# Attention over a sparse graph, edge by edge in place of dense with a mask

## The chip, the cores and the metric

The kernel runs on one core of a Trainium2 chip. The core has five engines with queues of their own: PE (TensorE, matmuls and transposes into PSUM), DVE (VectorE), ACT (ScalarE), POOL (GpSimd) and SP (SyncE, which issues DMAs here). Instructions stand in order on each engine and wait for one another through semaphores. The metric is the device time of one execution in microseconds (us), lower is better. Timed runs are not profiled; one further execution is profiled, and every duration below comes from it.

## What is computed

One layer of a graph neural network: layer norm and relu of x, then attention with 8 heads of 64 over the neighbours that `adj` allows, and x is added back. x is (16, 1024, 512) float32, `adj` is (1024, 1024) and the same for all 16 batches.

```
h = maximum(layernorm(x), 0)
q, k, v = (h @ W + b).reshape(b, n, 8, 64)            # for Wq, Wk, Wv of 512 x 512
scores = einsum('bihd,bjhd->bhij', q, k) / sqrt(64)
scores = scores + where(adj == 0, -1e9, 0)
out = einsum('bhij,bjhd->bihd', softmax(scores), v)
return x + out.reshape(b, n, 512)
```

The inputs make an adjacency with hubs: an edge (i, j) has the chance 0.0039 w_i w_j with w falling as the root of the index, and each token has an edge to itself. With the seed used there are 5,061 edges among 1,048,576 pairs; the token with the most has 66, the median token 4.

## The kernel before

`main_path` (lines 37 to 309) does the dense attention. A batch has 8 iterations of the loop at line 300: one for each of 4 pairs of heads (128 columns) and each half of 512 queries. An iteration goes over 8 tiles of 128 keys in `scores` (line 169): two matmuls of 64 rows by 512 queries (line 174), the mask added by DVE from PSUM (line 177), the exponential on ACT (line 178), and a running sum over the key tiles on POOL (lines 181 and 183). `weighted_sum` (line 185) multiplies with V for the iteration before (line 192), reduces the running sum on DVE (line 202), and loads the piece of x to be added. `row_sums` and `finish` (lines 212 and 224) make the inverse, transpose back on PE (line 229), divide on DVE (line 231), add x on POOL (line 236) and store from SP's queue (line 237).

The work of the next batch is spread over the iterations as fillers (line 245): x is loaded, `stats` takes mean and variance on DVE (lines 116 to 118) and the power on POOL (line 119), `norm` makes the shift on DVE (line 125) and the relu on ACT (line 126), `flip` transposes on PE (line 135) and copies on ACT (line 136), and `proj_k`, `proj_q` and `proj_v` do four matmuls of 512 columns each with a bias added (lines 143, 150 and 159). The order on PE, DVE, ACT and POOL inside this loop is the order in which the code is written (`manual_schedule`, line 299); only SP's is chosen by the scheduler.

`make_mask` writes the mask once, transposed by PE. Since no maximum is subtracted ahead of the exponential, `all_rows_fine` looks at the row sums at the end, and only if one is out of bounds does `general_path` run over everything again.

Of the kernel before, what the change touches and what calls it, by code (L numbers as in the profile page):

```python
# [19 lines left out]
F32 = mybir.dt.float32  # L21
BF16 = mybir.dt.bfloat16
# [12 lines left out]


def main_path(tc, x, adj, Wq, bq, Wk, bk, Wv, bv, out, sums):
# [4 lines left out]
    NH = N // 512  # L42
    TH = NT // NH
    DC = D // P
    ITS = DC * NH

    with ExitStack() as ctx:
        pool = lambda name, bufs=1, **k: ctx.enter_context(tc.tile_pool(name=name, bufs=bufs, **k))
        const = pool("const")
        xpool = pool("xpool", 5)  # L50
        hpool = pool("hpool", 4)
        kqpool = pool("kqpool", 2)
        vpool = pool("vpool", 2)
        ppool = pool("ppool", 12)
        apool = pool("apool", 2)
        work = pool("work", 2)
        small = pool("small", 4)
        psum = bass.MemoryType.PSUM
        ps_s = pool("ps_s", 3, space=psum)
        ps_a = pool("ps_a", 2, space=psum)  # L60

        X, HT, Q, K, V, MV, RSTD = {}, {}, {}, {}, {}, {}, {}

        def load_x(b, t):
            X[b, t] = xpool.tile([P, D], F32, tag="x", name=f"x_{b}_{t}")
            nc.sync.dma_start(X[b, t], x[b, ts(t, P), :])

        for t in range(2):
            load_x(0, t)

        ident = const.tile([P, P], F32, tag="ident", name="ident")
        make_identity(nc, ident)

        same = const.tile([P, P], F32, tag="same", name="same")
        own = const.tile([P, 2 * TH, 4], F32, tag="own", name="own")
        place = const.tile([P, 32], F32, tag="place", name="place")
        group = const.tile([P, 4], F32, tag="group", name="group")
        nc.vector.tensor_reduce(place, ident.rearrange("p (g q) -> p q g", q=32), AX.X, ALU.add)
        nc.vector.tensor_reduce(group, ident.rearrange("p (g q) -> p g q", q=32), AX.X, ALU.add)
        nc.vector.tensor_copy(same.rearrange("p (g q) -> p g q", q=32), place[:, None, :].to_broadcast([P, 4, 32]))  # L80
        nc.vector.tensor_copy(own, group[:, None, :].to_broadcast([P, 2 * TH, 4]))
        minus_half = const.tile([P, 1], F32, tag="mhalf", name="minus_half")
        nc.gpsimd.memset(minus_half, -0.5)

        W = {}
        bias = {}
        for name, w, vec in (("k", Wk, bk), ("q", Wq, bq), ("v", Wv, bv)):
            W[name] = const.tile([P, DC, H * HD], F32, tag="w" + name, name="w" + name)
            nc.sync.dma_start(W[name], w.rearrange("(c p) n -> p c n", p=P))  # L89
            if name == "v":  # L90
                bias[name] = const.tile([P, H * HD], F32, tag="bv", name="bv_rows")
                src = bass.AP(tensor=vec.tensor, offset=vec.offset, ap=[[0, P], [1, H * HD]])
            else:
                bias[name] = const.tile([P, DC], F32, tag="b" + name, name=f"b{name}_cols")
                src = vec.rearrange("(c p) -> p c", p=P)
            nc.sync.dma_start(bias[name], src)  # L96


        mask = const.tile([P, NT, N], BF16, tag="mask", name="mask")

        def make_mask(qt):
            row = ppool.tile([P, N], F32, tag="p", name=f"adj_{qt}")
            nc.sync.dma_start(row, adj[ts(qt, P), :])
            nc.vector.tensor_scalar(row, row, 0.0, -BIG * HD**0.5, op0=ALU.is_equal, op1=ALU.mult)
            for g in range(NT // 4):
                pt = ps_a.tile([P, 4, P], F32, tag="acc", name=f"pmask_{qt}_{g}")
                for j in range(4):
                    nc.tensor.transpose(pt[:, j, :], row[:, ts(4 * g + j, P)], ident)  # L108
                nc.scalar.copy(mask[:, 4 * g : 4 * g + 4, ts(qt, P)], pt)
# [381 lines left out]
```

## Time and profile before

| | us |
|---|---|
| median of 3 runs (3400.69 to 3402.33) | 3401.33 |
| the profiled execution, its own time | 3402.22 |
| its span | 3400.4 |
| ACT, activations of line 178: busy | 1082.3 |
| DVE, mask of line 177: busy | 1182.2 |
| POOL, running sum of lines 181 and 183: busy | 302.9 + 1811.3 |

The page of a profile gives for each engine the busy time in the span, the chain of work that ended last (followed back from the last instruction, with shares by engine and line), and groups of instructions: line, engine, operation, output<-inputs with their shapes, count | busy time in us, mean ns of one | idle time of the engine just ahead of them and what ended it. Windows give the busy time of each engine in a stretch, the granted TensorE clock, the DMA engines' busy share and GB/s. A float32 matmul can have more than one record for one instruction of the program, so records are set against the loops of the code.

### The profile page before, as it was taken

What the parts mean: (1) busy time and instruction counts of PE and PEld (TensorE: products, weight loads), DVE (VectorE), ACT (ScalarE), POOL (GpSimd) and SP (SyncE); (2) the same over time, 40 slices, a digit from 0 to 9 for tenths busy, and PEclk for the clock granted to TensorE, in tenths of its full rate; (3) what the DMA queues carried; (4) which work ended last, traced back from release to release, by engine and by line L of the source; (5) the groups of instructions that cost most, each with busy time, mean ns of one, the idle gap of its engine ahead of it and who ended that gap; (6) DMA issues with size and microseconds to landing.
All of it is one profiled execution on the core that took longest, in us unless ns stands there. A gap on an engine that the chain in (4) does not pass through costs nothing.

```text
span 3400.4 us, 33496 instructions
## 1 busy us (share of the span) xinstructions
PE 3359.0 (99%) x12610; PEld 1365.5 (40%) x12610; DVE 1998.0 (59%) x2450; ACT 1414.9 (42%) x1553; POOL 2338.3 (69%) x1160
## 2 busy tenths in 40 slices
PE   7999999999999999999999999999999999999997
PEld 3344444444443444344434443444444434444433
DVE  3556556565665656656556565665566556565455
ACT  3444434444443444344444443444444434444343
POOL 0777767676776677667666776777677767676777
PEclk9999999999999999999999999999999999999999
DMA  3011101111010111001100010101101110110000
GB/s 136 28 28 33 34 28 28 34 32 32 25 38 25 32 31 35 28 25 31 38 28 29 25 41 28 28 28 35 31 29 30 36 28 29 32 31 19 19 25 26
DMA packets 157704, 110.49 MB, mean 32 GB/s; under 512 B 7392, under 2 KB 138464, under 8 KB 157536
## 3 DMA queue, kind: packets, MB, share of 16 engines
q1 hardware_dynamic: 157536, 108.30, 10.7%
q8 instruction: 100, 1.64, 0.2%
q14 instruction: 68, 0.56, 0.1%
HBM read 74.72 MB, written 33.55 MB: 32 GB/s over the span
## 4 chain that ended last, share of the span: by engine, by line
PE 97%; DVE 1%; POOL 1%; issue 1%; SPq 0%; DMA 0%; ACT 0%; DVEq 0%; POOLq 0%; ACTq 0%
PE ps L174 27%; PE po L192 26%; PE pq L150 13%; PE pk L143 13%; PE pv L159 13%; PE pht L135 2%; PE pot L229 2%; PE pr L215 1%; POOL a L183 1%; DVE p L177 0%; PE pmask L108 0%; DMA x<-in_x_dram 0%; SPq L89 0%; DVE st L116 0%; SPq L96 0%
## 5 line engine op out<-in xcount | busy, mean ns | idle before, releaser
L183 POOL TENSOR_TENSOR a<-a,p 128x1024 f32<-128x1024 f32 x768 | 1811.3, 2359 | 782.8 <-ACT p L178 732.6
L177 DVE TENSOR_TENSOR p<-ps,mask 128x1024 f32<-128x1024 f32 x1024 | 1182.2, 1217 | 750.7 <-PE ps L174 750.7
L178 ACT ACTIVATE p<-p 128x1024 f32<-128x1024 f32 x1024 | 1082.3, 1057 | 770.8 <-DVE p L177 714.4
L174 PE MATMUL ps<-qT,kT 64*128 64x512 f32 x4096 | 953.2, 603 | 5.3 <-DVE p L177 5.2
L192 PE MATMUL po<-p,v 128*64 128x512 f32 x4096 | 907.1, 595 | 1.5 <-DVE picked L219 1.5
L174 PEld LDWEIGHTS ps<-qT,kT 64*128 64x128 f32 x4096 | 365.1, 186 | 486.7 <-issue 346.2
L192 PEld LDWEIGHTS po<-p,v 128*64 128x64 f32 x4096 | 282.8, 137 | 609.7 <-issue 540.4
L181 POOL TENSOR_TENSOR a<-p,p 128x1024 f32<-128x1024 f32 x128 | 302.9, 2366 | 237.4 <-ACT p L178 237.4
L204 ACT COPY ot<-po 128x512 f32<-128x512 f32 x128 | 75.0, 586 | 938.9 <-PE po L192 938.9
L150 PE MATMUL pq<-hT,wq 128*128 128x512 f32 x1024 | 464.4, 596 | 0.0
L143 PE MATMUL pk<-hT,wk 128*128 128x512 f32 x1024 | 455.3, 597 | 0.0
L159 PE MATMUL pv<-wv,hT 128*128 128x512 f32 x1024 | 454.4, 597 | 0.0
L159 PEld LDWEIGHTS pv<-wv,hT 128*128 128x128 f32 x1024 | 189.9, 190 | 215.7 <-issue 215.7
L143 PEld LDWEIGHTS pk<-hT,wk 128*128 128x128 f32 x1024 | 189.7, 190 | 215.2 <-issue 215.0
L150 PEld LDWEIGHTS pq<-hT,wq 128*128 128x128 f32 x1024 | 184.5, 190 | 212.2 <-issue 198.5
L151 DVE TENSOR_SCALAR qT<-pq,bq_cols 128x512 f32<-128x512 f32 x128 | 96.1, 751 | 235.0 <-PE pq L150 235.0
L125 DVE SCALAR_TENSOR_TENSOR shift<-mv,rstd 128x1 f32<-128x1 f32 x128 | 226.3, 1777 | 2.6 <-POOL rstd L119 2.6
L231 DVE TENSOR_TENSOR o<-pot,inv 128x512 f32<-128x512 f32 x128 | 87.9, 686 | 190.6 <-PE pot L229 190.2
L160 DVE TENSOR_TENSOR v<-pv,bv_rows 128x512 f32<-128x512 f32 x128 | 87.9, 687 | 170.6 <-PE pv L159 170.6
L126 ACT ACTIVATE x<-x,shift,rstd 128x512 f32<-128x512 f32 x128 | 102.3, 811 | 174.7 <-DVE shift L125 174.5
L236 POOL TENSOR_TENSOR o<-o,xr 128x512 f32<-128x512 f32 x128 | 163.4, 1277 | 0.6 <-DVE o L231 0.6
L202 DVE TRANSPOSE_TENSOR_REDUCE rs<-a 128x32 f32<-128x1024 f32 x128 | 158.0, 1234 | 9.8 <-POOL a L183 9.8
(40 smaller groups left out, 845.5 us busy)
## 6 DMA issues: line engine op xcount, KB each, us to landing
x<-in_x_dram SPq DMA_DIRECT2D x128, 256.0 KB, 3.1
xr<-in_x_dram SPq DMA_DIRECT2D x128, 256.0 KB, 3.1
out_dram<-o SPq DMA_DIRECT2D x128, 256.0 KB, 2.4
adj<-in_adj_dram SPq DMA_DIRECT2D x8, 512.0 KB, 7.1
wk<-in_L_gnn_Wk_dram SPq DMA_DIRECT2D x1, 1024.0 KB, 8.7
wq<-in_L_gnn_Wq_dram SPq DMA_DIRECT2D x1, 1024.0 KB, 10.5
wv<-in_L_gnn_Wv_dram SPq DMA_DIRECT2D x1, 1024.0 KB, 11.9
bv_rows<-in_L_gnn_bv_dram SPq DMA_DIRECT2D x1, 256.0 KB, 8.6
```

The lines of the kernel that those rows point to most:

```text
L125: nc.vector.scalar_tensor_tensor(shift, mv[:, 0:1], -1.0, rstd, op0=ALU.mult, op1=ALU.mult)
L143: nc.tensor.matmul(acc, W["k"][:, c, ts(p, P)], HT[b, hf][:, c, :], start=(c == 0), stop=(c == DC - 1))
L150: nc.tensor.matmul(acc, W["q"][:, c, ts(p, P)], HT[b, hf][:, c, :], start=(c == 0), stop=(c == DC - 1))
L159: nc.tensor.matmul(acc, HT[b, hf][:, c, ts(tt, P)], W["v"][:, c, :], start=(c == 0), stop=(c == DC - 1))
L174: nc.tensor.matmul(ps[:, r, :], K[b, p][rows, ts(kt, P)], Q[b, p, qh][rows, :], start=True, stop=True)
L177: nc.vector.tensor_tensor(pr, ps, m[:, None, :].to_broadcast([P, 2, 512]), ALU.add)
L178: nc.scalar.activation(pr, pr, AF.Exp, scale=HD**-0.5)
L181: nc.gpsimd.tensor_tensor(ACC[i], PR[i, 0], pr, ALU.add)
L183: nc.gpsimd.tensor_tensor(ACC[i], ACC[i], pr, ALU.add)
L192: nc.tensor.matmul(po[rows, :], V[b][:, kt, p * P + r * HD : p * P + r * HD + HD], pr[:, r, :], start=(kt == 0), stop=(kt == NT - 1),)
L202: nc.vector.tensor_reduce(RS[i], acc, AX.X, ALU.add, apply_transpose=True)
L236: nc.gpsimd.tensor_tensor(o, o, XR.pop(i), ALU.add)
```

## The change

The dense attention on the main path is replaced by one that touches only edges. The dense general path stays behind the check at the end.

Once, before the loop: the degree of each token is counted, tokens are ranked by degree (highest first) with comparisons on DVE, and `perm` lists the tokens in this order. All later tiles of 128 tokens are in sorted order. The rows of `adj` are fetched in this order by indirect DMA, and each row's neighbours are found as the largest entries of a row that holds 1024 - rank where there is an edge (`max` gives eight at a time; `match_replace` removes them for the tile of the hubs). Tile t keeps at most `CAPS[t]` neighbours a token; a hub's further neighbours are cut in pieces of 5, and 128 extra rows ("tile -1") hold one piece each; the matrix `owner` says whose. Slots without a neighbour point to row 1023 and get the mask. The number of used slots and of edges go into `cover`, which the check at the end compares.

In each batch: x is fetched in sorted order by indirect DMA; statistics, relu, transposes and projections are as before in kind, but K and V (bias added on DVE for both) are stored to a DRAM tile of 1024 rows of 1024 floats, and q is projected when its tile comes. Then 11 units follow, each some slots of a tile: `gather` issues one indirect DMA a slot on POOL (128 rows of 4 KB: K and V of a neighbour), `score` multiplies K with q, reduces over 64 to 8 heads and adds the mask on DVE, then the exponential on ACT; `weigh` multiplies V with the weights, on ACT for units 0, 1 and 2 (one activation for each slot and head), on DVE for the others; `add_up` sums the slots by matmuls with the identity into PSUM, or, for units 5, 8 and 9, by a reduce on DVE and one matmul; `finish` sums the weights, divides, adds x on POOL, and scatters the rows to `out` by indirect DMA from POOL. There are three buffers for gathered rows. A unit's `weigh` and `add_up` are written after the `score` of the next one.

```
+CAPS = (11, 8, 6, 5, 4, 4, 3, 2)
+PIECE = 5
+PIECES = 17
...
+UNITS = ((7, 0, 2), (6, 0, 3), (5, 0, 4), (4, 0, 4), (3, 0, 5), (2, 0, 6), (1, 0, 4), (1, 4, 4), (0, 0, 6), (-1, 0, 5), (0, 6, 5))
...
+        gpool = pool("gpool", 3)
...
+        def load_x(n):
+            b, t = tile_at(n)
+            X[n] = xpool.tile([P, D], F32, tag="x", name=f"x_{b}_{t}")
+            nc.gpsimd.indirect_dma_start(
+                out=X[n][:], out_offset=None, in_=x_rows, in_offset=on(ap=perm[:, t : t + 1], axis=0), element_offset=b * N * D
+            )
...
+        def proj_kv(n):
...
+            for j, name in enumerate("kv"):
+                pt = ps_kv.tile([P, D], F32, tag="pkv", name=f"p{name}_{b}_{t}")
+                project(pt, name, n)
+                nc.vector.tensor_tensor(kv[:, j, :], pt, bias[name], ALU.add)
+            nc.sync.dma_start(KV[b][ts(t, P), :], kv.rearrange("p j d -> p (j d)"))
...
+        def gather(i):
...
+            G[i] = gpool.tile([P, UMAX, 2, D], F32, tag="g", name=f"g_{b}_{u}")
+            for s in range(count):
+                nc.gpsimd.indirect_dma_start(
+                    out=G[i][:, s].rearrange("p j d -> p (j d)"),
+                    out_offset=None,
+                    in_=KV[b][:],
+                    in_offset=on(ap=index[:, c + s : c + s + 1], axis=0),
+                )
...
+        def score(i):
...
+            k = G[i][:, :count, 0, :]
+            nc.vector.tensor_tensor(k, k, Q[b, t][:, None, :].to_broadcast([P, count, D]), ALU.mult)
...
+            nc.vector.tensor_reduce(w, k.rearrange("p s (h d) -> p s h d", h=H), AX.X, ALU.add)
+            nc.vector.tensor_tensor(w, w, mask[:, c : c + count, None].to_broadcast([P, count, H]), ALU.add)
+            nc.scalar.activation(w, w, AF.Exp, scale=HD**-0.5)
...
+        ON_ACT = (0, 1, 2)
...
+            if u in ON_ACT:
+                for s in range(count):
+                    for h in range(H):
+                        nc.scalar.mul(v[:, s, h, :], v[:, s, h, :], w[:, s, h : h + 1])
+            else:
+                nc.vector.tensor_tensor(v, v, w[:, :, :, None].to_broadcast([P, count, H, HD]), ALU.mult)
+
+        BY_REDUCE = (5, 8, 9)
...
+            if u in BY_REDUCE:
+                r = work.tile([P, D], F32, tag="r", name=f"r_{b}_{u}")
+                nc.vector.tensor_reduce(r, v.rearrange("p s d -> p d s"), AX.X, ALU.add)
+                terms = [r]
+            else:
+                terms = [v[:, s, :] for s in range(count)]
+            for k, term in enumerate(terms):
+                nc.tensor.matmul(
+                    acc,
+                    owner_t if t < 0 else ident,
+                    term,
...
+        def ahead(n):
+
+            if n + 3 < tiles:
+                load_x(n + 3)
+            if n + 2 < tiles:
+                stats(n + 2)
+            if n + 1 < tiles:
+                flip(n + 1)
+            proj_kv(n)
+            if n + 2 < tiles:
+                norm(n + 2)
...
+        LEAD = 2
+        with tc.manual_schedule(engines={mybir.EngineType.PE, mybir.EngineType.DVE, mybir.EngineType.Activation, mybir.EngineType.Pool}):
+            go_ahead(NT + LEAD)
...
             for i in range(total):
...
+                score(i)
+                if i:
+                    weigh(i - 1)
+                go_ahead(NT * (b + 1) + LEAD + NT * passed // SLOTS)
...
+                        queries(nb, nt)
+                if i:
+                    add_up(i - 1)
+                if i + 2 < total:
+                    gather(i + 2)
...
+                        finish(pb, home)
```

Three places show how the engines' order moves. In the rows a number after x is a count of like instructions in a row; names are the tiles of the code, with a number that tells buffers apart.

POOL before, one iteration in the middle of the program (`a` is the running sum of the weights `p`, `o` the result to which x is added):

```order
L236 TENSOR_TENSOR o_2440<-o_2440,xr_2373 128x512
L181 TENSOR_TENSOR a_2456<-p_0_2447,p_1_2453 128x1024
L183 TENSOR_TENSOR a_2456<-a_2456,p_2_2461 128x1024
L183 TENSOR_TENSOR a_2456<-a_2456,p_3_2468 128x1024
L119 TENSOR_TENSOR rstd_1_2504<-rstd_1_2504,minus_half 128x1
L183 TENSOR_TENSOR a_2456<-a_2456,p_4_2516 128x1024
```

POOL of the changed kernel, two units in the middle of the second batch (`g` is the buffer of a unit, `x` a tile in sorted order):

```order
L306 DMA g_4_1459<-kv_628,index 128x1024 x5
L386 TENSOR_TENSOR o_6_1469<-o_6_1469,x_6_544 128x512
L387 DMA out_dram<-o_6_1469,perm 16384x512
L154 DMA x_1_1510<-in_x_dram,perm 128x512
L166 TENSOR_TENSOR rstd_2_1514<-rstd_2_1514,minus_half 128x1
L306 DMA g_5_1555<-kv_628,index 128x1024 x6
```

The running sums are gone from POOL, and what SP issued before (loads of x, stores of the result) stands there now, with the gathers, in one queue with the power and the addition of x.

DVE of the changed kernel, from the mask of unit 2 to the division of the tile before it, whose weighing is on ACT:

```order
L323 TENSOR_TENSOR w_5_2020<-w_5_2020,mask 128x32
L163 BN_STATS st_3_2050<-x_3_1894 128x6
L164 BN_AGGR mv_3_2051<-st_3_2050 128x2
L165 TENSOR_SCALAR rstd_3_2052<-mv_3_2051 128x1
L198 TENSOR_TENSOR kvt_5_2064<-pk_5_2065,bk_rows 128x512
L198 TENSOR_TENSOR kvt_5_2064<-pv_5_2071,bv_rows 128x512
L173 SCALAR_TENSOR_TENSOR shift_3_2078<-mv_3_2051,rstd_3_2052 128x1
L298 TENSOR_TENSOR pq_4_2082<-pq_4_2082,bq_rows 128x512
L369 TENSOR_REDUCE sums<-w_6_1977 128x8
L377 TENSOR_SCALAR sums<-sums 128x8
L379 RECIPROCAL inv_6_2100<-sums 128x8
L381 TENSOR_TENSOR o_6_2102<-acc_6_2088,inv_6_2100 128x512
```

Before, eight instructions of line 177 stood in each iteration and the division followed a transpose; now the division (line 381) stands behind the next unit's score and waits for PE's sum of the unit before.

PE before, in one iteration (`po` is the weighted sum):

```order
L135 MATMUL pht_3_3946<-ident,x_3_3574 128x128 x4
L150 MATMUL pq_1_1_3953<-hT_1_3016,wq 128x512 x4
L192 MATMUL po_3959<-p_0_3788,v_2833 64x512 x2
L192 MATMUL po_3959<-p_1_3794,v_2833 64x512 x2
L192 MATMUL po_3959<-p_2_3802,v_2833 64x512 x2
```

PE of the changed kernel, two units (`acc` is the sum of a tile's slots):

```order
L182 MATMUL pht_4_1424<-ident,h_4_1293 128x128 x4
L188 MATMUL pk_5_1432<-wk,hT_5_1275 128x512 x4
L188 MATMUL pv_5_1438<-wv,hT_5_1275 128x512 x4
L188 MATMUL pq_4_1449<-wq,hT_4_796 128x512 x4
L359 MATMUL acc_6_1455<-g_1_1304,ident 128x512 x3
L182 MATMUL pht_3_1519<-ident,h_3_1447 128x128 x4
L188 MATMUL pk_4_1527<-wk,hT_4_1429 128x512 x4
```

The scores and the dense weighted sum are gone; a unit's sum (line 359) stands behind the projection of a tile of the next batch and of the next q, and ahead of the next transposes.

More of the change, by code (lines that the diff above doesn't have):

```diff
@@ L75, in main_path @@
[L75 to L80, printed above, removed]
@@ L224, in finish, with project @@
[L224 to L230 removed]
+            HT[n] = htpool.tile([P, DC, P], F32, tag="hT", name=f"hT_{b}_{t}")
+            nc.scalar.copy(HT[n], pt)
+        def project(pt, name, n):
+            for c in range(DC):
+                nc.tensor.matmul(pt, HT[n][:, c, :], W[name][:, c, :], start=(c == 0), stop=(c == DC - 1))
@@ new lines, in main_path, with queries @@
+        Q, G, WT, ACC = {}, {}, {}, {}
+        def queries(b, t):
+            pt = ps_q.tile([P, D], F32, tag="q", name=f"pq_{b}_{t}")
+            if t >= 0:
+                project(pt, "q", nth(b, t))
+                HT.pop(nth(b, t))
+            else:
+                nc.tensor.matmul(pt, owner, Q[b, 0], start=True, stop=True)
+                Q[b, t] = pt
+                return
+            if t == 0:
+                q = Q[b, t] = work.tile([P, D], F32, tag="q0", name=f"q0_{b}")
+            else:
+                q = Q[b, t] = pt
+            nc.vector.tensor_tensor(q, pt, bias["q"], ALU.add)
```

452 lines of the change are left out of this document (248 added, 204 removed).

## The prediction

> **What bounds the kernel now.** Read first the busy shares and the chain of the profile's page, then its groups of instructions.
>
> ```profile
> span 3400.4 us, 33496 instructions
> PE 3359.0 (99%) x12610; PEld 1365.5 (40%) x12610; DVE 1998.0 (59%) x2450; ACT 1414.9 (42%) x1553; POOL 2338.3 (69%) x1160
> ...
> PE 97%; DVE 1%; POOL 1%; issue 1%; SPq 0%; DMA 0%; ACT 0%; DVEq 0%; POOLq 0%; ACTq 0%
> ...
> L174 PE MATMUL ps<-qT,kT 64*128 64x512 f32 x4096 | 953.2, 603 | 5.3 <-DVE p L177 5.2
> L192 PE MATMUL po<-p,v 128*64 128x512 f32 x4096 | 907.1, 595 | 1.5 <-DVE picked L219 1.5
> ...
> L143 PE MATMUL pk<-hT,wk 128*128 128x512 f32 x1024 | 455.3, 597 | 0.0
> ```
>
> TensorE is busy 99% of the span and makes up 97% of the chain: the time is PE's work. 953 + 907 = 1860 us of it are the dense scores and the dense weighted sum, over all 1024 x 1024 pairs of tokens, of which the mask leaves 5,061. The change can only win there. One unit is needed for the rest: line 143 is reached 512 times (16 batches, 4 head pairs, 2 halves, 4 chunks of D), and the row counts 1024 records and 455.3 us, so a 128x512 float32 matmul of the program costs **0.89 us** of PE.
>
> The whole main path is replaced, so I build the new time from its stages. The sum is held against the profiled execution, 3402.2 us with a span of 3400.4; the median of the runs is 3401.33, the same within 0.03%.
>
> **DVE per batch.** A batch now is 11 units with 48 slots; a slot is 128 gathered rows.
>
> ```profile
> L177 DVE TENSOR_TENSOR p<-ps,mask 128x1024 f32<-128x1024 f32 x1024 | 1182.2, 1217 | 750.7 <-PE ps L174 750.7
> L160 DVE TENSOR_TENSOR v<-pv,bv_rows 128x512 f32<-128x512 f32 x128 | 87.9, 687 | 170.6 <-PE pv L159 170.6
> L231 DVE TENSOR_TENSOR o<-pot,inv 128x512 f32<-128x512 f32 x128 | 87.9, 686 | 190.6 <-PE pot L229 190.2
> L116 DVE BATCH_NORM_STATS2 st<-x 128x6 f32<-128x512 f32 x128 | 84.1, 657 | 14.9 <-DMA x<-in_x_dram 14.9
> L222 DVE RECIPROCAL inv<-sums 128x8 f32<-128x8 f32 x128 | 26.0, 203 | 4.5
> L220 DVE TENSOR_REDUCE sums<-picked 128x8 f32<-128x32 f32 x128 | 23.8, 186 | 4.4
> L117 DVE BATCH_NORM_AGGREGATE mv<-st 128x2 f32<-128x6 f32 x128 | 23.2, 182 | 4.2
> L118 DVE TENSOR_SCALAR rstd<-mv 128x1 f32<-128x1 f32 x128 | 19.6, 153 | 4.3
> L425 DVE TENSOR_REDUCE c_both<-sums 128x1 f32<-128x1024 f32 x1 | 1.2, 1210 | 0.0
> L78 DVE TENSOR_REDUCE place<-ident 128x32 f32<-128x128 f32 x1 | 0.4, 358 | 0.0
> L79 DVE TENSOR_REDUCE group<-ident 128x4 f32<-128x128 f32 x1 | 0.3, 276 | 0.0
> ```
>
> 512 elements take 687 ns and 1024 take 1217: 0.53 us for each 512 and 0.155 us an instruction; the reduce fits (1210). So: q times K, 48 slots in 11 instructions, 48 x 0.53 + 11 x 0.155 = 27.1. The reduce to 8 heads, the same, 27.1. Weights times V for the units that stay on DVE, 39 slots in 8, 21.9. Summing by reduce in units 5, 8 and 9, 17 slots in 3, 9.5, with strided reading: line 78 takes 82 ns more than line 79 for the same 128 elements, at most 0.64 ns each, so between 0 and 5.6 more; I take 2. Bias of K and V, 16 x 0.687 = 11.0; of q 5.5; division 8 x 0.686 = 5.5. Statistics 8 x (0.657 + 0.182 + 0.153) = 7.9 and the shift 1.2; mask, sums, clamps, reciprocals (0.15 to 0.2 each) 6.8. Together **125.5 us**, against 1998 / 16 = 125 before: DVE gains nothing.
>
> **PE per batch.** K, V and q of 8 tiles, 96 matmuls, one for the moved queries, 34 for the sums: 131 x 0.89 = 116.6, plus 32 transposes.
>
> ```profile
> L135 PE MATMUL pht<-ident,x 128*128 128x128 f32 x512 | 87.1, 296 | 20.6 <-ACT x L126 20.3 <-ACT hT L136 0.3
> ```
>
> These cost 87.1 / 512 = 0.17 each, 5.4. Together **122 us**, where it was 3359 / 16 = 210.
>
> **POOL and the DMA queues per batch.** POOL issues 48 gathers, 8 loads of x and 8 scatters, all 64 indirect DMAs that no row shows.
>
> ```profile
> L183 POOL TENSOR_TENSOR a<-a,p 128x1024 f32<-128x1024 f32 x768 | 1811.3, 2359 | 782.8 <-ACT p L178 732.6
> L236 POOL TENSOR_TENSOR o<-o,xr 128x512 f32<-128x512 f32 x128 | 163.4, 1277 | 0.6 <-DVE o L231 0.6
> L119 POOL TENSOR_TENSOR rstd<-rstd,minus_half 128x1 f32<-128x1 f32 x128 | 69.9, 550 | 30.7 <-DVE rstd L118 30.7
> ...
> 1.68 0.43 SPq L89 DMA_DIRECT2D wk<-in_L_gnn_Wk_dram  x1
> ...
> 8.11 1.94 SPq L96 DMA_DIRECT2D bv_rows<-in_L_gnn_bv_dram  x1
> ...
> 16.00:18.00 2.00, 0.00 (x0) 0.00 (x0) 0.61 (x1) 0.00 (x0) 0.00 (x0) 1.00 1.06 406
> 32.00:34.00 2.00, 1.91 (x14) 1.34 (x14) 1.00 (x2) 1.67 (x4) 0.00 (x0) 1.00 1.04 398
> ```
>
> Bounds for one issue: 0.43 us (SP's, of a plain load) to 2.36 (POOL's longest row). I take 1.28, POOL's row for one 128x512 tile, since 128 addresses have to be worked out by that engine. POOL: 64 x 1.28 + 8 x (1.277 + 0.55) = 96.5 us. The accumulations of line 183 go. Bytes: 48 x 0.52 + 8 x (0.26 + 0.52 + 0.26) = 33.6 MB a batch; both windows of full queues move about 400 GB/s, and the first still carries bv_rows, one 2 KB row read 128 times (issued at 8.11), as the padding here reads row N-1. That is 84 us. The stores of K and V wait in SP's queue for DVE; only later stores stand behind them.
>
> So no engine has more than 126 us in a batch, where before it was 210. What remains is who waits for whom. A gather waits on POOL for its buffer, freed by the sum three units earlier; behind it stand the add of x, the scatter, the next load and the next power, for which DVE's shift waits, but DVE first has a score to do (5 to 7 us), which covers it.
>
> **Waits on DVE, the first: ACT.** In units 0, 1 and 2 the weighing is 16, 24 and 32 activations of 64 elements.
>
> ```profile
> L178 ACT ACTIVATE p<-p 128x1024 f32<-128x1024 f32 x1024 | 1082.3, 1057 | 770.8 <-DVE p L177 714.4
> L204 ACT COPY ot<-po 128x512 f32<-128x512 f32 x128 | 75.0, 586 | 938.9 <-PE po L192 938.9
> L126 ACT ACTIVATE x<-x,shift,rstd 128x512 f32<-128x512 f32 x128 | 102.3, 811 | 174.7 <-DVE shift L125 174.5
> ...
> 6.31 1.52 ACT L126 ACTIVATE x<-x,shift,rstd 128x512 f32<-128x512 f32 x2 [1.35 <-DVE shift L125]
> ```
>
> 1024 against 512 elements is 0.47 us, so 64 with a scale per partition take about 0.811 - 0.41 = 0.40; two in a row start 0.71 apart, 0.1 less: 0.30 (bounds 0.17, from line 204's fixed part, and 0.40). That is 4.8, 7.2 and 9.6 us, then 2, 3 and 4 matmuls (1.8, 2.7, 3.6), before DVE can divide. In between DVE has 1.2 us of its own (q bias, small reduces) after unit 0 and 3.8 (statistics and K/V bias too) after the others: it waits 5.4 + 6.1 + 9.4 = **21 us**. **The second: PE in turns.** In a unit with a tile to project PE has 0.7 + 7.1 + 3.6 + about 4 = 15 us, DVE 12 to 14. About 2 us in six units, and 3 for the small matmul of finish(b, 0) that stands behind a projection: **15 us**.
>
> **The third: DVE against POOL.**
>
> ```profile
> 1999.22 2.19 DVE L125 SCALAR_TENSOR_TENSOR shift<-mv,rstd 128x1 f32<-128x1 f32 x1
> ...
> 1999.04 7.22 POOL L183 TENSOR_TENSOR a<-a,p 128x1024 f32<-128x1024 f32 x3
> ...
> L125 DVE SCALAR_TENSOR_TENSOR shift<-mv,rstd x128: 145/2182/2255, 6.1 to 3121.2; 128x1 f32<-128x1 f32 x128
> ```
>
> The shift has two SBUF operands and one element: 145 ns at best, 2.19 us here, ending as POOL's first addition ends. About 30 such instructions a batch remain (masks, weighing, shifts). If an indirect issue holds them as an addition does, 30 x half of 1.28 x POOL's share 0.6 is 11 us; if not, none. I take **4**. The Trainium skill, SBUF — State Buffer, section Who interferes with whom, says that a two-input DVE instruction contends only with a GpSimd instruction that reads SBUF. By that the additions hold it, as the 2.19 us show, and an issue that reads no tensor would not: the term would be 0 and the time 64 us less.
>
> **The fourth: PE's rate after idle.**
>
> ```profile
> 2003.71 0.60 PE L229 MATMUL pot<-ident,ot 128*128 128x128 f32 x4
> ...
> 3388.65 0.61 PE L215 MATMUL pr<-rs,same 128*128 128x32 f32 x2 [3.49 <-DVE rs L202]
> ...
> 3389.64 1.08 PE L229 MATMUL pot<-ident,ot 128*128 128x128 f32 x4 [0.38 <-DVE picked L219]
> ```
>
> Four transposes take 0.60 us in the stream and 1.08 after PE had been idle 3.49 us. PE will idle that long while ACT weighs, some four times a batch; a few us at half rate cost 1 to 2 us each time, mostly beside DVE: **5**.
>
> **The sum.** 125.5 + 21 + 15 + 4 + 5 = 170.5 us a batch, x 16 = 2728. Ahead of the loop, sorting and lists: 63 DVE instructions on 1024 elements at about 1.24, 45 small ones at 0.16, and some 15 us of loads and hand-overs, 100; then ten tiles of projection, PE 7.8 plus 1.5 of turns each, 93. The last batch projects nothing (-30), last store and check +10. 100 + 93 + 2728 - 30 + 10 = about **2900 us**.
>
> **The rivals.**
> - *Nearly no waiting.* ACT's multiplications at 0.17 and PE ahead of DVE: 140 us a batch, 2415. For it: four engines with slack. Against: one unit of lead, and PE and DVE within 4 us of each other. 0.20.
> - *POOL becomes the bound, slower than before.* Place: POOL's queue, 64 issues. With 15 us of buffer waits a batch is 64 c + 30; at c = 2.36 that is 181, 3070 us. It equals before where a batch takes (3402 - 173) / 16 = 202 us, c = 2.7; at 3.2 it is 235, 3930. For it: POOL's rows are the slowest per element. Against: nothing is added up. 0.15, 0.06 of it slower.
> - *PE stays at half rate.* With half of its matmuls at it PE needs 183 us, with 20 of waits 203 and 3420; with all, 244 and more. For it: the 1.08 against 0.60, and an engine that falls to 72% busy with gaps. Against: as it slows the gaps close. The Trainium skill, TensorE: Matmul & The Clock Gate, section HAM oscillation — how this bites in real kernels, says gaps over about 3.4 us drop the clock to half each time; the 3.49 us here agree, though the column of the granted clock reads 1.00. 0.09, 0.07 of it slower.
> - *Gathers at half bandwidth.* At 200 GB/s 168 us of transfers and 10 of waits, 3020; slower below 175 GB/s. Against: 398 and 406 in both full windows. 0.08, 0.03 slower.
> - *The sparse path isn't taken.* More edges than slots would add the dense general path to all this. The seed's adjacency has 5,061 edges, tile maxima of 66, 8, 6, 5, 4, 3, 3, 2 (caps 11 and extra pieces, 8, 6, 5, 4, 4, 3, 2) and 101 of 128 extra pieces: it fits. 0.02.
>
> **How the numbers follow.** My forecast, 2900 within 200, has 0.46. The range reaches down into the first rival and up into the others: 2450 to 3450 leaves out some 0.2. Slower: 0.06 + 0.07 + 0.03 + 0.02 = 0.18; within 0.2% (7 us, about what a measurement of this kernel can tell from no change) 0.03; faster 0.79.
>
> **What would show it.** DVE near 2000 us and PE near 1960 busy, neither above 75%; DVE idle before the division, released by PE's sums; the indirect issue on POOL near 1.3 us; L336 near 0.3 us; DMA share near a half. I am wrong in a step if POOL or the DMA leads the chain, if matmuls of 128x512 last clearly longer than 597 ns, or if a batch takes under 145 us.

## The result, and the profile after

The changed kernel takes **2872.61 us** (median of 4 runs, 2870.18 to 2873.86) where the kernel before takes 3401.01 beside it: a ratio of 0.8446, 95% interval 0.8431 to 0.846. The forecast was 2900, within 2450 to 3450.

The page of the changed kernel, the same parts as were shown of before:

```profile
span 2872.0 us, 16724 instructions
PE 2074.3 (72%) x4759; PEld 912.0 (32%) x4759; DVE 2161.5 (75%) x2287; ACT 485.2 (17%) x1590; POOL 1462.3 (51%) x1298
...
PEclk9998898888989888888989888897988889798776
...
q0 software_dynamic: 132224, 474.02, 49.3%
...
PE 43%; DVE 36%; issue 8%; ACT 6%; DMA 6%; POOL 1%; DVEq 0%; SPq 0%; ACTq 0%; POOLq 0%
```

PE was 99% busy and 97% of the chain. Now no engine is busy more than 75%, and the chain changes hands between PE and DVE. The granted clock is mostly at eight or nine tenths and ends at six; before, it was at nine or more in every slice:

```profile
PEclk9999999999999999999999999999999999999999
```

The queue of POOL's DMAs (the gathers, and the loads of x and scatters with them) takes 49% of the DMA engines.

The groups of instructions, with shapes apart, in the same columns:

```profile
L306 POOL DMA_INDIRECT g<-kv,index x768 | 865.9, 1127 | 988.1 <-PE acc L359 418.1 <-DVE r L354 227.6 <-issue 184.7
L336 ACT ACTIVATE g<-g,w 128x64 f32<-128x64 f32 x1152 | 280.0, 333 | 0.6 <-ACT w L324 0.2
L354 DVE TENSOR_REDUCE r<-g 128x512 f32<-128x3072 f32 x32 | 170.5, 5327 | 0.6
L322 DVE TENSOR_REDUCE w<-g 128x48 f32<-128x3072 f32 x32 | 107.3, 3353 | 1.1
L359 PE MATMUL acc<-r,ident 128*128 128x512 f32 x64 | 65.9, 1133 | 460.4 <-DVE sums L369 242.3 <-DVE r L354 218.1
L323 DVE TENSOR_TENSOR w<-w,mask 128x32 f32<-128x32 f32 x64 | 59.4, 928 | 2.2
L323 DVE TENSOR_TENSOR w<-w,mask 128x40 f32<-128x40 f32 x32 | 6.4, 200 | 1.1
```

Three rows stand out. The strided sum (L354) needs 5.33 us for 3072 elements where the reduce along rows (L322) needs 3.35: 0.64 ns more an element. The matmul that takes its result is at 1133 ns a record, almost twice the 600 of the stream, after 460 us of idle time. And the mask of 32 elements takes 928 ns, of 40 elements 200.

Nine batches: the window runs from PE's small matmul for the moved queries (ahead of unit 9) in the first batch, at 307.1 us, to the same matmul in the tenth, at 1812.5, which is 167.3 us for each. First the busy time of PE, PEld, DVE, ACT and POOL, granted clock, DMA share and GB/s; then what DVE waited for:

```profile
307.10:1812.50 1505.40, 1152.59 (x2666) 508.73 (x2665) 1169.16 (x1207) 269.97 (x891) 820.76 (x721) 0.87 0.59 201
```

```profile
DVE o L381 <- PE acc L359: 111.4, 54, 5.3
DVE shift L173 <- POOL rstd L166: 80.5, 45, 4.6
DVE pq L298 <- PE pq L188: 56.5, 27, 2.7
DVE sums L375 <- PE p_more L374: 30.4, 9, 3.4
DVE g L318 <- DMA g<-kv,index: 25.8, 9, 3.5
DVE q L298 <- PE pq L188: 7.0, 9, 1.0
DVE kvt L198 <- PE pv L188: 5.5, 18, 1.4
```

DVE works 1169 / 9 = 129.9 us a batch and waits (317.1 us in these rows) 35.2; 2 us are small gaps. That the rows add up to the batch says nothing yet of which of them is worth anything: a wait that goes may only make room for the next. The experiments ask that.

### The profile page after: what moved, and what is told of

It reads as the page before. It is cut to its first block, busy times and chain, and to the rows that moved or that the text cites. A ratio compares the mean times of both kernels' runs of the same rounds, so it can differ in the third digit from the quotient of the medians.

```text
span 2872.0 us, 16724 instructions
## 1 busy us (share of the span) xinstructions
PE 2074.3 (72%) x4759; PEld 912.0 (32%) x4759; DVE 2161.5 (75%) x2287; ACT 485.2 (17%) x1590; POOL 1462.3 (51%) x1298
## 4 chain that ended last, share of the span: by engine, by line
PE 43%; DVE 36%; issue 8%; ACT 6%; DMA 6%; POOL 1%; DVEq 0%; SPq 0%; ACTq 0%; POOLq 0%
PE acc L359 13%; PE pq L188 10%; PE pk L188 9%; PE pv L188 8%; DVE g L318 8%; DVE r L354 8%; DVE w L322 7%; DVE g L338 5%; ACT g L336 5%; DMA g<-kv,index 5%; PE pht L182 2%; DVE w L323 1%; POOL g L306 1%; DVE st L163 1%; ACT h L175 1%
## 5 line engine op out<-in xcount | busy, mean ns | idle before, releaser
L306 POOL DMA_INDIRECT g<-kv,index x768 | 865.9, 1127 | 988.1 <-PE acc L359 418.1
L359 PE MATMUL acc<-g,ident 128*128 128x512 f32 x992 | 500.4, 646 | 111.0 <-ACT g L336 64.5
L188 PE MATMUL pk<-wk,hT 128*128 128x512 f32 x1024 | 497.2, 631 | 0.0
L188 PE MATMUL pq<-wq,hT 128*128 128x512 f32 x1024 | 489.1, 623 | 0.0
L359 PE MATMUL acc<-r,ident 128*128 128x512 f32 x64 | 65.9, 1133 | 460.4 <-DVE sums L369 242.3
L322 DVE TENSOR_REDUCE w<-g 128x32 f32<-128x2048 f32 (+4 forms) x160 | 391.4, 2446 | 5.5
L338 DVE TENSOR_TENSOR g<-g,w 128x2048 f32<-128x2048 f32 (+2 forms) x112 | 306.9, 2740 | 0.0
L318 DVE TENSOR_TENSOR g<-g,pq 128x2048 f32<-128x2048 f32 (+4 forms) x128 | 291.5, 2278 | 0.1
L336 ACT ACTIVATE g<-g,w 128x64 f32<-128x64 f32 x1152 | 280.0, 333 | 0.6 <-ACT w L324 0.2
L381 DVE TENSOR_TENSOR o<-acc,inv 128x512 f32<-128x512 f32 x128 | 88.6, 692 | 226.2 <-PE acc L359 223.8
L354 DVE TENSOR_REDUCE r<-g 128x512 f32<-128x3072 f32 (+1 forms) x48 | 241.9, 5039 | 0.6
L387 POOL DMA_INDIRECT out_dram<-o,perm x128 | 207.6, 1622 | 37.3 <-POOL o L386 35.3
## 6 DMA issues: line engine op xcount, KB each, us to landing
wq<-in_L_gnn_Wq_dram SPq DMA_DIRECT2D x1, 1024.0 KB, 12.4
```

Of the source, the lines that this page charges most:

```text
L188: nc.tensor.matmul(pt, HT[n][:, c, :], W[name][:, c, :], start=(c == 0), stop=(c == DC - 1))
L306: nc.gpsimd.indirect_dma_start(out=G[i][:, s].rearrange("p j d -> p (j d)"), out_offset=None, in_=KV[b][:], in_offset=on(ap=index[:, c + s ...
L318: nc.vector.tensor_tensor(k, k, Q[b, t][:, None, :].to_broadcast([P, count, D]), ALU.mult)
L322: nc.vector.tensor_reduce(w, k.rearrange("p s (h d) -> p s h d", h=H), AX.X, ALU.add)
L336: nc.scalar.mul(v[:, s, h, :], v[:, s, h, :], w[:, s, h : h + 1])
L338: nc.vector.tensor_tensor(v, v, w[:, :, :, None].to_broadcast([P, count, H, HD]), ALU.mult)
```

## The experiments

Each is an edit of the changed kernel. Ratios are against the kernel before, with their 95% intervals; differences are against 2872.61.

**Weighing on DVE.**

```
-        ON_ACT = (0, 1, 2)
+        ON_ACT = ()
```

> Units 0 to 2 are weighed by DVE instead of ACT. Theory 1 (DVE waits for ACT's 72 small activations through PE's sums): DVE gets 9 slots more, 9 x 0.53 + 3 x 0.155 = 5.2 us a batch, and loses the wait before the division (223.8 us in all, 14 a batch): 8.8 x 16 = 141 us less, about 2730 us; the L381 idle falls under 60 us. Rival A (DVE's work is the bound and the wait is only slack that other waits would fill): 5.2 x 16 = 83 us more, about 2955. Rival B (the wait moves to another hand-over, PE's projections): within 30 us of 2873.

Measured: 2834.11 us, 0.8334 (0.832 to 0.8348): 38 less, a quarter of theory 1. DVE's busy time rose by 77 us (to 2238.9), where 83 were priced, but the wait before the division only fell to 148 us. Added up by tile from the timelines, it fell from 155.7 to 80.5 us in units 0 to 2, so ACT was only part of the reason for PE's sum to be late there:

```profile
L381 DVE TENSOR_TENSOR o<-acc,inv 128x512 f32<-128x512 f32 x128 | 88.5, 692 | 151.2 <-PE acc L359 148.3 <-DMA x<-in_x_dram,perm 0.9
```

All of DVE's waits together fell from 667 to 549 us, so without ACT's weighing DVE waits 118 / 16 = 7 us a batch less.

**Sums on PE.**

```
-        BY_REDUCE = (5, 8, 9)
+        BY_REDUCE = ()
```

> Units 5, 8 and 9 are summed by PE (17 matmuls a batch instead of 3 and 3 strided reduces on DVE). Theory 1 (the slow strided reduces, 241.9 us on DVE, leave PE idle for 460 us before its sums and cold after it): DVE loses 15.1 us a batch, PE gains 14 x 0.89 = 12.5 that mostly fill its idle time: between 100 and 200 us less, about 2730; the matmuls after it go back from 2.04 to 1.8 us a pair or better. Rival A (PE is the bound): 12.5 x 16 = 200 us more, 3070. Rival B (DVE and PE just change places, one saving what the other adds): within 40 us of 2873.

Measured: 2770.62 us, 0.8145 (0.8132 to 0.8159): 102 less. Theory 1 holds against "PE is the bound". DVE is busy 262 us less, PE 153 more, though 14 x 0.89 x 16 = 199 were added: the rest of PE's matmuls got faster, with a granted clock of 0.92 for 0.87. But DVE's waits rose by 157 us, over half of it before the division (223.8 to 309.7).

**PE kept busy.** Filling matmuls into a PSUM tile that nothing reads:

```
+        FILL = {5: 14, 8: 12, 9: 4}
...
+            if u in FILL:
+                for k in range(FILL[u]):
+                    nc.tensor.matmul(pt, ident, W["q"][:, 0, :], start=True, stop=True)
```

> Ahead of the sums of units 5, 8 and 9 PE does 14, 12 and 4 matmuls whose result nobody reads, in time in which it waits for DVE's reduce (15.2, 13.1 and 5.2 us of idle in batch 7). Theory 1 (PE's slow rate after the idle stretches is on the path): the sum of r goes from 1133 to about 500 ns a record (64 records, 40 us), and of the 4 transposes and 8 K or q matmuls behind them 0.5 and 1.5 us go, two or three times a batch: 40 to 120 us less in all, 2750 to 2830. Rival (DVE is late there whatever PE's rate is; the slow matmuls are covered by DVE's next work): within 15 us of 2873, though the same matmuls get faster in the trace. If the filling overruns the idle time it costs up to 2 us in each unit, 30 to 60 us more.

Measured: 2830.4 us, 0.8318 (0.8304 to 0.8332): 42 less, with 960 records of filling added. DVE's waits fell by 27 us, and its busy time by 14, all of it in masks (L323) that happened to meet fewer additions of x. So PE's slow rate is on the path. The timelines show where it was and what is left of it (start, duration, instructions, idle before); first the changed kernel, then the run with filling:

```profile
1456.58 2.04 PE L359 MATMUL acc<-r,ident 128*128 128x512 f32 x2 [15.15 <-DVE sums L369]
1458.42 1.06 PE L182 MATMUL pht<-ident,h 128*128 128x128 f32 x4
1459.27 5.07 PE L188 MATMUL pk<-wk,hT 128*128 128x512 f32 x8
1464.18 3.60 PE L188 MATMUL pv<-wv,hT 128*128 128x512 f32 x8
```

```profile
1435.12 1.22 PE L368 MATMUL acc<-r,ident 128*128 128x512 f32 x2 [3.19 <-DVE sums L378]
1436.13 1.06 PE L182 MATMUL pht<-ident,h 128*128 128x128 f32 x4
1436.99 4.79 PE L188 MATMUL pk<-wk,hT 128*128 128x512 f32 x8
...
1484.77 2.08 PE L368 MATMUL acc<-r,ident 128*128 128x512 f32 x2 [3.29 <-DVE r L363]
```

After 15 us of idle the pair of records takes 2.04 us, the transposes 1.06 for 0.60, and K's matmuls 5.07 for 3.60. The granted clock, asked in windows of a microsecond, follows this: in the changed kernel it is 0.50 from 1446 to 1462 us and 1.00 from 1463 on. The filling left gaps ahead of the sums, 1.8 to 3.3 us in 45 of the 48 places, and the clock still falls behind the longer ones. It is 0.50 from 1436 to 1439 us in the first place above, where the pair (1.22 us) was nearly through by then, and from 1484 to 1490 in the second (2.08). In 12 of the 13 places with a gap of 2.30 to 3.13 us the pair took 2.05 to 2.08 us; in the 15 places with 1.78 to 1.91 us it took 1.12 or 1.13. So some of the slow rate is left, and 42 us needn't be all that it costs.

The Trainium skill, TensorE: Matmul & The Clock Gate, section HAM oscillation — how this bites in real kernels, puts the gap that drops the clock at over about 3.4 us; here gaps from 2.3 us were enough, and the measurement decides. The Trainium skill, TensorE: Matmul & The Clock Gate, section What's actually happening, has the window over which activity is watched running freely, which may be why gaps as alike as 3.19 and 3.29 us end differently; no run here shows the window itself.

**Half of the bytes.**

```
-                KV[b] = dram.tile([N, 2 * D], F32, tag="kv", name=f"kv_{b}")
+                KV[b] = dram.tile([N, D], F32, tag="kv", name=f"kv_{b}")
...
-                    out=G[i][:, s].rearrange("p j d -> p (j d)"),
+                    out=G[i][:, s, 1, :],
...
```

The lines left out store K alone and let the score read the gathered rows where they now lie; K's rows stand for V's too.

> Only the K half of a row is stored and gathered (2 KB instead of 4 KB for each of 128 rows); K's rows stand for V's too, so the output is another. Number of instructions on all engines as before. Theory 1 (transfers are covered but for the 47.3 us in which DVE waits for a gather in unit 9): 0 to 50 us less, 2825 to 2873. Rival A (the gathers' transfer sets the pace, their share of the 16 DMA engines being 49%): some 80 us x 16 x 0.4, over 300 us less. Rival B (cost per row, not per byte): nothing moves, also unit 9's wait stays, and the share of the queue stays near 49%.

Measured: 2869.1 us, 0.8436 (0.8422 to 0.845): 3.5 less, no difference to be told. The queue's share fell to 32.2%, DVE's wait for gathers from 47.3 to 3.3 us, and nothing came of it: DVE's waits fell by 26 in all, and its busy time rose by 20, of which 18 are in the masks of L323. With the gather early, unit 9's mask meets POOL's addition of x, and takes 1.32 us for 0.20:

```profile
1323.06 1.28 POOL L386 TENSOR_TENSOR o<-o,x 128x512 f32<-128x512 f32 x1
...
1323.10 1.32 DVE L323 TENSOR_TENSOR w_-1_5007<-w_-1_5007,mask 128x40 f32<-128x40 f32 x1
```

Transfers are covered. The 44 us of waiting for gathers that went brought 3.5: 18 came back as other waits, 18 as masks that meet an addition.

**Shift one tile later.**

```
             if n + 1 < tiles:
-                flip(n + 1)
+                norm(n + 1)
             proj_kv(n)
-            if n + 2 < tiles:
-                norm(n + 2)
+            if n + 1 < tiles:
+                flip(n + 1)
...
```

> DVE's shift and ACT's normalization of a tile are put one tile later (ahead of the next tile's K and V, the transposes behind them), so that POOL's power has a whole tile's time. The row of waits of the shift (131.6 us, 75 times) should fall under 20 us. Theory 1 (what DVE waits, the batch waits, since nothing in the queue behind it can start): 110 to 130 us less, about 2755. Rival (PE sets the pace at these places, and DVE's saved wait comes back as a wait for K, V or q from PE, as in the run with half of the bytes, where 44 us of waits went and 3.8 us of the time): within 30 us of 2873.

Measured: 3409.9 us, 1.0028 (1.0019 to 1.0038): 537 **more**, and outside both theories. The wait that the edit was aimed at is gone, and another has come:

```profile
PE pht L182 <- ACT h L175: 547.0, 118, 27.7
```

```profile
1420.46 2.29 DVE L322 TENSOR_REDUCE w<-g 128x32 f32<-128x2048 f32 x1
1421.39 3.60 PE L188 MATMUL pv<-wv,hT 128*128 128x512 f32 x8
...
1424.10 5.84 ACT L336 ACTIVATE g<-g,w 128x64 f32<-128x64 f32 x24
...
1424.77 0.15 DVE L173 SCALAR_TENSOR_TENSOR shift<-mv,rstd 128x1 f32<-128x1 f32 x1
...
1429.85 0.80 ACT L175 ACTIVATE h<-x,shift,rstd 128x512 f32<-128x512 f32 x1
1430.70 1.11 PE L182 MATMUL pht<-ident,h 128*128 128x128 f32 x4 [5.72 <-ACT h L175]
```

I had given up the tile of lead between the normalization and the transposes. PE is done with V at 1425.0; its transposes wait for h, which stands behind 24 weighings in ACT's queue (from 1424.10 on), and behind the transposes stands q, for which DVE waits (608.8 us, where it was 96.1).

**Division one unit later.**

```
-                if i:
-                    pb, pu = divmod(i - 1, NU)
+                if i > 1:
+                    pb, pu = divmod(i - 2, NU)
```

> The division, the addition of x and the store of a tile are done one unit later, so that PE's sum has a unit's time. The wait before the division (223.8 us) should go to under 40 us, and POOL's addition comes earlier in relation to its queue. Theory 1 (the waits of the division are on the path): 150 to 220 us less, 2650 to 2720. Rival (PE is late and only the place changes where DVE notices it): the waits for K, V, q and p_more grow by most of what is saved, and the time is within 50 us of 2873.

Measured: 2775.59 us, 0.8158 (0.8145 to 0.8172): 97 less, between the theories. The wait before the division (223.8 us) is gone entirely, but shift, gathers, K and V wait 68, 50 and 48 us more; DVE's waits fell only from 667 to 624. The other 60 us are DVE's busy time: the mask of 128x32 takes 194 ns for 928, and all masks together 35.5 us for 97.0, since POOL's addition of x now falls beside other instructions.

**No addition of x.**

```
-            nc.gpsimd.tensor_tensor(o, o, X.pop(nth(b, t)), ALU.add)
+            X.pop(nth(b, t))
```

> POOL's addition of x (128 instructions of 1.29 us) is left out, so the output lacks x. Theory 1 (that addition holds DVE's two-input instructions, as 1.09 and 1.33 us of L323 ending with it show): the mean of L323 on 128x32 falls from 928 to about 200 ns, 62 us of DVE's busy time go and some of the shift's wait behind POOL's queue too: 60 to 120 us less, about 2780. Rival A (an indirect issue holds DVE just as well): L323 stays above 600 ns. Rival B (DVE's hold is hidden, PE being late): L323 falls, but the time stays within 25 us of 2873.

Measured: 2808.4 us, 0.8261 (0.8247 to 0.8275): 64 less; theory 1 holds, at its lower end.

```profile
L323 DVE TENSOR_TENSOR w<-w,mask 128x32 f32<-128x32 f32 x64 | 13.5, 211 | 2.2
```

The mask is back at 211 ns, while POOL still issues all gathers: an issue doesn't hold DVE, the addition does. DVE's busy time is 61 us less, its waits 3. So the shorter masks were paid in full here. (The edit also takes the addition out of POOL's queue: the shift's wait fell by 49 us, but the other waits rose by nearly as much.)

**Three edits together**: sums on PE, shift later, division later.

> Sums of units 5, 8 and 9 by PE, shift one tile later and division one unit later, together. PE has 2227 us of work in the run with sums on PE. Theory 1 (the waits are separate and add up): from 2770 the 310 us before the division and the 167 before the shift go: about 2300 to 2350, and PE is above 90% busy. Theory 2 (PE, 139 us a batch, becomes the bound): 193 + 16 x 139 = 2417 plus some waits, 2420 to 2550. Rival (the waits are one wait seen at three places): above 2650.

Measured: 3141.4 us, 0.923 (0.9197 to 0.9263). It looks like the rival, but PE waits 485 us for h again, so this run says nothing of the other two edits. The next two separate them.

**Power one tile earlier.** The other way to give POOL time, with the lead kept:

```
-            if n + 3 < tiles:
-                load_x(n + 3)
-            if n + 2 < tiles:
-                stats(n + 2)
+            if n + 4 < tiles:
+                load_x(n + 4)
+            if n + 2 < tiles:
+                norm(n + 2)
...
-            if n + 2 < tiles:
-                norm(n + 2)
+            if n + 3 < tiles:
+                stats(n + 3)
...
```

There is one more buffer for x, and the first tiles are prepared to match.

> x is loaded and its statistics and POOL's power are done one tile earlier (one more x buffer); the normalization keeps its lead of a tile over the transposes, which the run with the shift one tile later had taken away (there PE waited 547 us for ACT's h). The shift's wait (131.6 us) should fall under 20 us, PE's wait for h stay near 57. Theory 1 (a wait of DVE is a wait of the batch): 100 to 130 us less, about 2755. Rival (DVE then waits for PE instead, as in the run with half of the bytes): within 30 us of 2873, and the waits of o, q, K and V grow by 80 to 130 us. If PE's wait for h grows again, slower by about that much.

Measured: 2849.3 us, 0.8379 (0.8365 to 0.8393): 23 less; the rival. (The profiled execution, 2839.52, is the fastest of the four, 10 us below the median.) The shift's wait falls from 131.6 us to under 10, and comes back at the places of PE (266.2 for 223.8, 79.2 for 35.9):

```profile
DVE o L381 <- PE acc L359: 266.2, 105, 7.4
DVE pq L298 <- PE pq L188: 105.5, 61, 2.4
DVE kvt L198 <- PE pv L188: 79.2, 66, 2.7
```

**Sums on PE and division later.**

> Sums of units 5, 8 and 9 on PE and the division one unit later, without the change of the shift. Theory 1 (the two waits are separate: DVE's before the division, and PE's before the sums of r): their gains of 102 and 97 us add up, 2674, or more, since the wait before the division had grown to 310 us in the run with sums on PE and all of it can go: 2560 to 2680. Rival A (the run with three waits gone was slow because the waits are one): above 2740. Rival B (that run was slow only because the transposes stood behind the late h): as theory 1, and PE's wait for h under 110 us.

Measured: 2676.25 us, 0.7868 (0.7852 to 0.7884): 196 less, the 102 and 97 added up. PE's wait for h is 57 us, as in the changed kernel, so the run of three, which had these two edits and the later shift, lost its time by the shift.

**All four**: with ACT's weighing on DVE and the power a tile earlier as well.

> Sums of units 5, 8 and 9 on PE, weighing of units 0 to 2 on DVE, division one unit later, statistics and power one tile earlier. DVE has 1900 + 83 = 1983 us of work, PE some 2200. Theory 1 (what is left are hand-overs that the two later places remove): PE leads, 193 + 139 x 16 = 2417 and some waits, 2430 to 2550. Rival (with PE and DVE at 139 and 115 us a batch and one unit of lead, each wait that goes is taken up by the next): 2600 to 2700. Not below 2400 by PE's work.

Measured: **2636.7 us**, 0.7748 (0.7735 to 0.7761): the fastest here, 8% below the changed kernel, but the rival's time. The last two edits give 40 us more. What leads now is the way of the buffers; POOL's and DVE's longest rows in the view of waits:

```profile
POOL g L306 <- PE acc L359: 399.6, 138, 12.2
```

```profile
DVE g L318 <- DMA g<-kv,index: 313.5, 87, 8.1
```

**Four gather buffers**, on top of all four edits, with units of at most 5 slots:

```
-        gpool = pool("gpool", 3)
+        gpool = pool("gpool", 4)
...
-UNITS = (..., (3, 0, 5), (2, 0, 6), (1, 0, 4), (1, 4, 4), (0, 0, 6), (-1, 0, 5), (0, 6, 5))
+UNITS = (..., (3, 0, 5), (2, 0, 3), (2, 3, 3), (1, 0, 4), (1, 4, 4), (0, 0, 4), (0, 4, 4), (-1, 0, 5), (0, 8, 3))
```

> As the run with all four edits, with units of at most 5 slots (13 units instead of 11 a batch, still 48 slots) and four gather buffers instead of three. Two units more cost DVE some 2 x (3 x 0.155 + 0.2 + 0.2) = 2 us a batch. Theory 1 (there the chain runs: PE's sum frees a buffer, POOL issues the unit's gathers at 1.25 us each, they land, DVE scores: POOL waits 400 us for PE's sums and DVE 313 us for gathers): with a buffer more POOL doesn't wait for the sum of the unit before, and DVE's wait for gathers falls under 120 us: 100 to 200 us less than 2637, 2440 to 2540. Rival (PE and DVE in turns are the rest, the gathers only stand in front of it): DVE's waits for q, K and V grow instead, 2600 to 2670.

Measured: 2663.61 us, 0.7832 (0.7819 to 0.7845): 27 more than with all four, the rival. POOL's wait for PE went from 400 to 60 us and DVE's for gathers from 313.5 to 131, and DVE waits for PE's projections instead (with three buffers 80.2 us for V and 83.2 for q). The run changes buffers and units at once, so it doesn't tell what either is worth alone:

```profile
DVE kvt L198 <- PE pv L188: 164.1, 70, 2.7
DVE pq L298 <- PE pq L188: 160.3, 106, 2.7
DVE g L318 <- DMA g<-kv,index: 131.0, 35, 7.7
```

**Read together.** Each run's span split into DVE's busy time and the sum of all rows of its view of waits (the 41 to 52 us that are left are small gaps):

| | span | DVE busy | DVE's waits |
|---|---|---|---|
| changed kernel | 2872.0 | 2161.5 | 667 |
| weighing on DVE | 2831.1 | 2238.9 | 549 |
| sums on PE | 2768.3 | 1899.7 | 824 |
| PE kept busy | 2832.3 | 2147.3 | 640 |
| half of the bytes | 2865.4 | 2181.3 | 640 |
| shift later | 3405.0 | 2189.7 | 1174 |
| division later | 2774.2 | 2101.9 | 624 |
| no addition of x | 2806.0 | 2100.2 | 664 |
| sums on PE, shift and division later | 3143.5 | 1878.2 | 1220 |
| power a tile earlier | 2837.7 | 2159.2 | 636 |
| sums on PE, division later | 2672.4 | 1896.9 | 727 |
| all four | 2642.9 | 1973.1 | 621 |
| all four, four buffers | 2659.3 | 1978.4 | 629 |

Leaving out the two runs with the later shift, edits that took a row of 130 to 310 us of waits away brought the sum of the waits down by 30 to 100 us (667 to 636 for the shift, 667 to 624 and 824 to 727 for the division), the fourth buffer not at all. Weighing on DVE, which shortens the way to PE's sum, brought 118, and DVE paid 77 of it. Of the 229 us between the changed kernel's span and the best one's, 188 are less work for DVE and 46 less waiting.

## Why the prediction was right

The mechanism was: dense work for 1,048,576 pairs goes, PE falls from 210 us a batch to about 122 and DVE stays at 125; then the batch is DVE's work plus what it waits for. That is what the profile shows. Its terms, in us a batch, measured over the nine batches:

| step | forecast | measured |
|---|---|---|
| DVE's work | 125.5 | 126.0 |
| held by POOL | 4 | 3.9 |
| waiting for ACT, at the division | 21 | 12.4, in one batch looked at 9.2 of it in units 0 to 2 |
| PE in turns (q, K, V, p_more) | 15 | 11.0 |
| PE's half rate, seen by DVE | 5 | in the rows above; filling brought 2.6, of it 0.9 in masks |
| shift, waiting for POOL's power | 0 | 8.9 |
| waiting for a gather | 0 | 2.9 |
| a batch | 170.5 | 167.3 |

- **DVE's work.** Right in sum by two errors: the strided sums cost 136 / 9 = 15.1 us where 11.5 was taken. The bound from line 78 (at most 0.64 ns an element) was the value, not an end; the rest was overestimated by as much.
- **The first wait, ACT.** Too large. ACT's activation starts every 0.24 us, not 0.30, and the step laid the sums one behind the other after ACT's last one, while PE begins when the first slot is weighed. One row of each engine in unit 0 of a batch:

```profile
1542.20 3.93 ACT L336 ACTIVATE g<-g,w 128x64 f32<-128x64 f32 x16
1544.27 3.70 PE L359 MATMUL acc<-g,ident 128*128 128x512 f32 x4 [3.85 <-ACT g L336]
1548.01 0.69 DVE L381 TENSOR_TENSOR o<-acc,inv 128x512 f32<-128x512 f32 x1 [3.27 <-PE acc L359]
```

  PE's 3.70 us hold a wait for the second slot, which ACT has done at 1546.13. Without ACT's weighing DVE waits 7 us a batch less, a third of the forecast.
- **The second, PE in turns.** Right in place and near in size.
- **The third, the hold.** Right in size. It isn't 30 instructions that wait for a part of an issue each, but the masks that meet an addition of x, in a batch looked at 4 of the 11 (units 1, 2, 6 and 7), for about a microsecond each (1.07 to 1.33 us in place of 0.2). Over nine batches the masks took 35.3 us more than 0.2 us each. The prediction inferred from the Trainium skill, SBUF — State Buffer, section Who interferes with whom, that an issue would not hold DVE; the run without the addition agrees (211 ns). Its zero for the term was too low all the same, since the additions alone, which that sentence names, make the 4 us; without them the time is 64 us less.
- **The fourth, half rate.** Real, and on the path, but not where it was put. Unit 0 has it (the four records above last 1.14 us in the median, for 0.59), but the long idle times are PE's waits for the strided sums of units 5, 8 and 9, which cost twice: DVE's time and then PE's rate. The forecast weighed the reduces as DVE's work alone. PE's busy time shows it, 1152.59 / 9 = 128.1 for 122. One reading was wrong: beside the 3.49 us of idle time of the kernel before, the column of the granted clock does not read 1.00. It reads 0.50 from 3388 to 3391 us; the 1.00 stands in the two windows near the start.
- **The shift's wait for POOL's power, "covered".** The step that was wrong. POOL's power stands behind the addition of x and the scatter, and DVE waited for the shift in most tiles, 8.9 us a batch. It cost little: with that wait gone the time fell by 23 us, 1.5 a batch, since DVE then waited for PE. A wait priced at nothing, and worth almost nothing, but not for the reason given.
- **POOL and DMA.** Right. An issue took 0.945 us in the median and 0.30 to the next one, 1.25 for the 1.28 taken (the mean is 1.127 us, since some are held, see below); half of the bytes changed nothing, and the queue's share was 49%.
- **Ahead of the loop**: the first bias of K starts at 103.2 us, for a forecast of 100, and the first unit's score at 194.3, for 193.
- **The signs.** DVE is busy 2161.5 us and PE 2074.3, where near 2000 and near 1960 were named. Those were the batches alone: up to 190 us DVE had worked 105 us and PE 85. Matmuls of 128x512 last 592 to 646 ns in the mean and 1133 behind the strided sums, for 597, so the sign of clearly longer matmuls was met in a part, which is the half rate above.

Of the rivals, half rate and POOL's bound didn't come. The clock's mean fell to 0.87; where it was asked by the microsecond it is at 1.00 or 0.50 but for the microseconds of a change, so the mean stands for (1 - 0.87) / 0.5, about a quarter of the time at half rate (an estimate), part of it with PE idle, as from 1446 to 1456 us. POOL is busy 51%. "Nearly no waiting" failed by the 35 us above. "Gathers at half bandwidth" looks met, at 201 GB/s and 167.3 us a batch where it named 200 and 168 of transfers; but with half of the bytes the time stayed, so the rate follows from the batch and doesn't set it.

The errors were of both signs: 12 us of waits were missed (shift and gathers), and up to 18 taken too many. That the sum is within 1% owes something to that, which is luck. It may also owe something to what the table of runs suggests: in this kernel the waits share one slack, so a misplaced wait moves the sum less than its row.

## What to carry to other kernels

Where two engines take turns in a unit and look one unit ahead, count the work of the engine that waits in full, but discount each wait: in this kernel removing one of 130 us brought 23, while 61 us of DVE's busy time brought 64, in one run each. Move an operation later only after asking who stands behind it in *every* queue: one normalization, one tile later, cost 537 us. A sum that leaves PE idle was paid twice here, by the engine that does it and by PE's rate afterwards.

## What the runs showed of the hardware

- **The hold works both ways.** Row pairs of the changed kernel's timeline; in the first DVE's mask waits for POOL's addition, in the second POOL's issue for DVE's weighing:

```profile
1446.47 1.27 POOL L386 TENSOR_TENSOR o<-o,x 128x512 f32<-128x512 f32 x1
1446.71 1.09 DVE L323 TENSOR_TENSOR w<-w,mask 128x32 f32<-128x32 f32 x1
...
1417.45 2.28 DVE L338 TENSOR_TENSOR g<-g,w 128x2048 f32<-128x2048 f32 x1
1417.59 2.96 POOL L306 DMA_INDIRECT g<-kv,index  x1 [0.30 <-issue]
```

  In the 500 us from 350 to 850, all 20 issues longer than 1.4 us began during a DVE instruction with two SBUF operands (17 times L338, 3 times L318 with q in SBUF) and ended 0.80 to 0.91 us after it. The Trainium skill, SBUF — State Buffer, section Who interferes with whom, tells of a probe in which `tensor_tensor` did not stall a DMA (the reason is marked there as inferred). The indirect issue here differs, 2.96 us for 0.945, and the measurement decides.
- **The clock gate and short gaps.** In the run with filling, PE's idle gaps of 1.8 to 1.9 us left the pair of records behind them at 1.12 us; behind 12 of 13 gaps of 2.3 to 3.1 us it took twice as long (2.05 to 2.08 us).
- **A strided reduce** costs 0.64 ns an element more than one along rows (5327 against 3353 ns for 3072).
